# Row loads of late full tiles, and the zeros behind the expert lists: other waits, another order

## The chip, the core and the metric

The kernel runs on one core of a Trainium2 chip. The metric is the device time of one execution in microseconds (us). TensorE is called PE here, VectorE DVE, ScalarE ACT, GpSimd POOL and SyncE SP, as the profile calls them. SP computes nothing in this kernel: its instruction queue issues most of the loads. POOL's queue issues the indirect (scattering) transfers.

## The reference, cut to what matters

One layer: a graph attention step over 4096 tokens of width 256 with a dense 4096 x 4096 adjacency, and then a mixture of 8 experts of which each token uses 2.

```
x = x + gat(layernorm(x), adj, ...)                     # 4 heads of 64, softmax over masked rows
xf = layernorm(x)
top_w, top_i = top_k(xf @ Wg + bg, 2);  top_w = softmax(top_w)
w_dense = sum(one_hot(top_i, 8) * top_w)
for e in range(8):
    h = gelu(xf @ W1[e] + b1[e])                        # 256 -> 1024
    out = out + w_dense[:, e] * (h @ W2[e] + b2[e])     # 1024 -> 256
x = x + out
```

The kernel does not multiply every token by every expert. It sorts tokens into one list for each expert and computes only those rows.

## The kernel before, in words

**Two stages.** The first stage is the attention. It goes over the tokens in four groups of 1024 rows (R). When a group's attention is summed, its rows are finished (residual, layer norm, gate), and each row is written twice, once into the list of each of its two experts. The lists lie in one DRAM tensor, `lists`, with a fixed stretch for each expert; a row is 256 values and four numbers (two weights, the token, the first expert). These writes are indirect DMAs from POOL at L1364, eight for a block of 512 tokens. The rows of the last group are not finished in the first stage: their two blocks (`last_block`) are interleaved, piece by piece, with the first expert tiles of the second stage, by `between`.

**Tiles of the second stage.** A tile is 256 rows of one expert. There are 27 in the main path, numbered here from 0 in the order of `todo`: 9 "early" tiles (0 to 8), which are full with rows of the first two groups alone; 8 "mid" tiles (9 to 16), full with rows of the first three groups alone; 8 "final" tiles (17 to 24), one for each expert, with up to 512 rows; and 2 more. Which expert and which place in its list a tile has is computed on the chip (`plan_early`, `plan_mid`, `plan_rest`), so SP loads a register from a table (L540) before it issues a load.

**One tile.** `fetch` issues three loads on SP: the second bias (L1767, 128 KB), the first weights w1 (L579 or `load_first`, 1 MB) and the second weights w2 (L1774, 1 MB), each with two buffers. `turn` transposes the rows (PE L586) and prepares indices and shares (DVE L1799 to L1816). `up` multiplies with w1 into 8 groups (PE L1848) and applies gelu (ACT L1852). `down` multiplies with w2 (PE L1882), scales (DVE L1895) and adds two blocks of 128 rows to the output by an indirect DMA on POOL (L1907).

**Row loads.** `load_full(k)` loads the 260 KB of rows of tile k on SP (L548, tile name `early`), into one of ROOM = 10 buffers. Tile 0 has its own buffer. Loads 1 to 10 are issued ahead of the loop over tiles. In the loop, iteration i of 2 or more issues the next: load 11 in iteration 2, up to load 16 in iteration 7. A row load waits by hand for every list write that is in `listed` when it is written down, and the framework also makes it wait for every earlier write to the `lists` tensor that was not declared independent.

**Zeros.** The final tiles read past the end of their lists, so zeros are written behind each list. `plan_rest`, reached in iteration 4 when the second last block is listed, writes all eight (POOL L497 to L502, 520 KB each) one after the other.

**Order.** [...] SP's queue holds, for each iteration, the loads of the tile ahead and one late row load, so a row load that waits holds up the weights behind it.

Of the kernel before, what the change touches and what calls it, by code (L numbers as in the profile page):

```python
# [29 lines left out]
CH = P  # L30
TT = 2 * CH
WT = 4 * CH
FINAL = (16, 15, 15, 15, 13, 13, 12, 9)
LIST = 36 * CH
# [10 lines left out]
def gat_then_moe(  # L45
# [19 lines left out]
    nc = tc.nc  # L65
    N, D = x.shape
    H, _, K = W.shape
    E, _, F = W1.shape
# [5 lines left out]
    HB = 2  # L74
# [4 lines left out]
    EARLY, BOTH = (-(-(2 * (N - k * R) - E * (TT - 1)) // TT) for k in (2, 1))  # L79
# [3 lines left out]
    ROOM = 10  # L83
# [5 lines left out]
    TB = B // P  # L89
# [17 lines left out]
    lists = nc.dram_tensor("lists", [E * LIST, RW], F32, kind="Internal").ap()  # L107
# [18 lines left out]
    token = numbers("token", [P, NT], [[P, NT]], step=1)  # L126
# [92 lines left out]
    def forward(apart, stack):  # L219
# [123 lines left out]
        early, mid, rest, final, over = tables("e", EARLY), {}, {}, {}, {}  # L343
# [95 lines left out]
        def plan_rest():  # L439

            plans[0] = kept
            rest.update(tables("r", LATE))
            n = moe_tile("nr", [P, E])
            nc.vector.tensor_tensor(n, filled, starts, OP.subtract)
            left = moe_tile("left", [P, E])
            nc.vector.scalar_tensor_tensor(
                left, used, -float(TT), n, op0=OP.mult, op1=OP.add
            )

            tiles = whole("r", left, TT - 0.5)  # L450
            nc.vector.tensor_scalar(tiles, tiles, -1.0, 0.0, op0=OP.add, op1=OP.max)
            plan(rest, LATE, n, tiles, used)
            nc.vector.tensor_tensor(used, used, tiles, OP.add)
            plan_final(n)
            counts = moe_tile("counts", [P, E + 3])
            above = counts[:, 3:]
            for i in range(E):
                nc.vector.tensor_scalar(
                    above[:, i : i + 1], final["rows"][:, i : i + 1], FINAL[i] * Q + 0.5, None,
                    op0=OP.is_gt,  # L460
                )
            nc.vector.tensor_copy(counts[:, 0:1], rest["upto"][:, E - 1 :])
            nc.vector.tensor_copy(counts[:, 2:3], strayed)
            more = moe_tile("more", [P, 2])
            nc.vector.tensor_scalar(more[:, 0:1], counts[:, 0:1], SURE + 0.5, None, op0=OP.is_gt)
            nc.vector.tensor_reduce(more[:, 1:2], counts[:, 2:], AX.X, OP.max)
            nc.vector.tensor_reduce(counts[:, 1:2], more, AX.X, OP.max)
            nc.vector.tensor_copy(count, counts)


            for t, name, chunks in (rest, "r", 2), (final, "f", 4):
                width = t["own"].shape[1]
                spare = moe_tile(f"spare{name}", [CH, width, chunks])
                nc.vector.tensor_copy(spare, inside[:, 0:1].unsqueeze(2).to_broadcast(spare.shape))
                theirs = moe_tile(f"theirs{name}", [CH, width])
                nc.vector.tensor_tensor(
                    t["past"], t["own"], others.unsqueeze(1).to_broadcast([CH, width, E]), OP.mult
                )
                nc.vector.tensor_reduce(theirs, t["past"], AX.X, OP.add)
                nc.vector.tensor_scalar(theirs, theirs, inside[:, 0:1], None, op0=OP.subtract)  # L480
                new = moe_tile(f"new{name}", [CH, width])
                nc.vector.tensor_scalar(new, t["place"], 0.0, None, op0=OP.is_equal)
                nc.vector.scalar_tensor_tensor(
                    new, t["expert"], float(E), new, op0=OP.is_lt, op1=OP.mult
                )
                nc.vector.tensor_tensor(theirs, theirs, new, OP.mult)
                nc.vector.tensor_tensor(
                    spare[:, :, :2], spare[:, :, :2],
                    theirs.unsqueeze(2).to_broadcast([CH, width, 2]), OP.add,
                )  # L490
                t["spare"] = spare
            zeros = moe_tile("zeros", [CH, WT // CH * RW])
            nc.gpsimd.memset(zeros, 0.0)
            ends = moe_tile("ends", [1, E], I32)
            nc.vector.tensor_copy(ends, filled[0:1, :])
            for e in range(E):
                end = nc.values_load(  # L497
                    ends[0:1, e : e + 1], engines=[mybir.EngineType.Pool],
                    min_val=e * LIST, max_val=e * LIST + N,
                    skip_runtime_bounds_check_because="a list holds each token at most once",  # L500
                )
                nc.gpsimd.dma_start(  # L502
                    lists[bass.ds(end, WT), :].rearrange("(p c) d -> p (c d)", p=CH), zeros
                )

        listed = []

        def after(ins, other, reason):
            tc.add_manual_dep(
                ins, other.name,  # L510
                mybir.DependencyInfo(mybir.DependencyClass.Sync, mybir.DependencyReason.DATA),
                reason=reason,
            )
# [28 lines left out]
                min_val=0, max_val=top, skip_runtime_bounds_check_because=why,  # L542
            )

        def load_rows_of(t, i, xr):
            rows = TT
            first = entry(t, 1, i, E * LIST - WT)
            ins = nc.sync.dma_start(  # L548
                xr, lists[bass.ds(first, rows), :].rearrange("(c p) d -> p c d", p=CH)
            ).ins  # L550
            for i in listed:
                after(ins, i, "rows of the tile")

        def rows_of_job(t, i):
            return FINAL[i] * Q if t is final else TT
# [38 lines left out]
        with ExitStack() as layer:  # L594
# [109 lines left out]
            sums = gat.tile([P, DC, NB], F32)  # L704
# [865 lines left out]
            def fresh():  # L1570

                last[0] = None
                listed.clear()

            def load_mask(a, j):
# [12 lines left out]
            if not apart:  # L1588

                with tc.tile_pool(name="gen", bufs=2) as work:  # L1590
# [12 lines left out]
                    for b in range(NB):  # L1603
                        mine = range(b * B, (b + 1) * B)
                        rows, top = er0[:, 0], er0[:, 1]
                        load_rows(er0[:, :1], b, 1, nc.scalar)
                        nc.vector.memset(top, -BIG)
                        for j in range(NT):
                            if j % 2 == 0:
                                at = load_adj(work, mine, j, 2, 2)  # L1610
# [15 lines left out]
                        for j in range(NT):  # L1626
                            if j % 2 == 0:
                                at = load_adj(work, mine, j, 2, 2)
# [115 lines left out]
        full_rows = [xr0]  # L1744
# [116 lines left out]
        def down(job, hT):  # L1861
# [26 lines left out]
            def give(k, size, po):  # L1888

                if job["last"]:  # L1890
                    o = kept.tile([CH, D], F32, name=f"o_last{k}")
                    last_sums.append(o)
                else:
                    o = work.tile([CH, D], F32, tag="o", name="o", bufs=2 * LAG - 3 if apart else 2)
                given_out.append(nc.vector.scalar_tensor_tensor(  # L1895
                    o[:size], po[:size], share[:size, k : k + 1], b2s[k][:size],
                    op0=OP.mult, op1=OP.add,
                ).ins)
                add = partial(
                    nc.gpsimd.indirect_dma_start, job["into"],  # L1900
                    bass.IndirectOffsetOnAxis(ap=ids[:size, k : k + 1], axis=0), o[:size], None,
                    compute_op=OP.add,
                )
                if job["last"]:
                    held_back.append(add)
                else:
                    add()  # L1907

            full, some = divmod(job["rows"], CH)
            split = some in (Q, 2 * Q)  # L1910
# [39 lines left out]
        def between(n):  # L1950
            if n == 0:
                begun.append(turn_sums(ud))
            for half in range(HB):
                if n == 2 * half:
                    begun.append(last_block(
                        b0 + half, u[:, half], begun[0][:, :, :, half], given[half],
                        xe[:, ts(half, TB)],
                    ))
                if n >= 2 * half and ordered[0]:
                    if next(begun[1 + half], "end") == "end" and half == HB - 1:  # L1960
                        ordered[0] = False
                        plan_rest()
# [8 lines left out]

        def load_full(i):
            xr = work.tile([CH, 2, RW], F32, tag="early", name="early", bufs=ROOM)
            load_rows_of(*((early, i) if i < EARLY else (mid, i - EARLY)), xr)
            full_rows.append(xr)

        for i in range(1, ROOM + 1):
# [7 lines left out]
        for i in range(len(todo)):  # L1985
            if i + 1 == len(jobs) and i + 1 < len(todo):
                jobs.append(fetch(*todo[i + 1]))
            nxt = jobs[i + 1] if i + 1 < len(todo) else None
            if i >= 2 and len(full_rows) < BOTH:
                load_full(len(full_rows))  # L1990
            hT = up(job, xT)
            between(2 * i)
            if nxt:
                xT = turn(nxt)
            giving = down(job, hT)
            next(giving)
            if nxt:
                next(giving, None)
            between(2 * i + 1)
            job = nxt  # L2000

        def held(k, top):
# [82 lines left out]
```

## Time and profile before

| | us |
|---|---|
| three runs | 1273.26, 1274.16, 1278.91 |
| median | 1274.16 |
| the profiled execution | 1281.52 |
| its span, first to last instruction | 1279.9 |
| attention stage, in the span | 0 to about 782 |
| expert tiles, in the span | about 782 to 1276 |

PE is busy for 97% of the span, DVE for 66%, ACT for 35% and POOL for 18%. The DMA engines moved 190.22 MB at a mean of 149 GB/s. In the profile a number such as L548 is a line of the kernel; "SPq" and "POOLq" are the instruction queues of SP and POOL, in which waits and issues of DMAs are recorded.

### The profile page before, as it was taken

To read this page: it belongs to the slowest core of one execution; us is meant where nothing else is said; L and a number is where in the kernel's file an instruction comes from. 1 tells how busy PE (TensorE), PEld (TensorE's weight loads), DVE (VectorE), ACT (ScalarE), POOL (GpSimd) and SP (SyncE) were. 2 spreads that over 40 slices of the span, in tenths; PEclk is the share of its full clock that TensorE was granted. 3 is DMA by queue.
4 is the path that set the end of the run, shared out by engine and by line. 5 is a ranking of instruction groups with operands and counts; after the bars stand their busy time and mean duration, and the time that the engine had idled before them with its cause. 6 is when DMAs were issued, how large, how long until landed. Compare 5 with 4: busy or idle time off the path is not lost.

```text
span 1279.9 us, 22496 instructions
## 1 busy us (share of the span) xinstructions
PE 1247.8 (97%) x8916; PEld 654.9 (51%) x8916; DVE 842.5 (66%) x1566; ACT 451.4 (35%) x929; POOL 235.0 (18%) x217
## 2 busy tenths in 40 slices
PE   8999999999999999999999999999699999999997
PEld 5444444332233322322334326887588886667676
DVE  7998887979999899999999985924011121111120
ACT  4332322165431465322644313432133332222322
POOL 4000000001004210016010051244222221222222
PEclk9999999999999999999999999999799999999999
DMA  6334433536434647335564325857866685555662
GB/s 211 116 116 153 128 100 105 193 83 174 151 105 121 209 106 210 109 97 175 134 195 125 118 72 184 255 161 236 252 177 164 192 211 130 105 113 126 139 148 46
DMA packets 131603, 190.22 MB, mean 149 GB/s; under 512 B 45560, under 2 KB 101744, under 8 KB 131104
## 3 DMA queue, kind: packets, MB, share of 16 engines
q1 hardware_dynamic: 109456, 145.39, 37.7%
q0 software_dynamic: 20544, 36.74, 13.0%
q10 hardware_dynamic: 1488, 6.55, 1.4%
q8 instruction: 72, 1.18, 0.4%
q14 instruction: 43, 0.35, 0.1%
HBM read 155.77 MB, written 29.74 MB: 145 GB/s over the span
## 4 chain that ended last, share of the span: by engine, by line
PE 90%; DVE 4%; issue 2%; DMA 2%; ACT 1%; POOL 1%; POOLq 1%; SPq 0%; DVEq 0%; ACTq 0%
PE acc L1177 33%; PE po L1882 17%; PE den L1186 16%; PE ph L1848 16%; PE pr L1032 2%; DVE w L1667 2%; PE ph L1080 2%; POOL lists L1364 1%; DMA w<-in_L_ffn_W 1%; PE pt L586 0%; PE ptx L1232 0%; DMA early<-lists 0%; PE acc L873 0%; DMA lists<-zeros 0%; PE pt L759 0%
## 5 line engine op out<-in xcount | busy, mean ns | idle before, releaser
L1177 PE MATMUL acc<-w,ha 128*32 128x512 f32 x4096 | 671.7, 593 | 2.5 <-issue 1.2
L1667 DVE SCALAR_TENSOR_TENSOR w<-er,eb,am 128x1024 f32<-128x1024 f32 x496 | 606.0, 1277 | 36.7 <-PE den L1186 30.3
L1186 PE MATMUL den<-w,unit 128*2 128x512 f32 x2048 | 467.4, 592 | 0.4 <-issue 0.3
L1177 PEld LDWEIGHTS acc<-w,ha 128*32 128x32 f32 x4096 | 186.4, 110 | 293.9 <-issue 254.5
L1584 ACT ACTIVATE am<-adj 128x1024 bf16<-128x1024 int32 x124 | 130.6, 1054 | 347.2 <-DVE w L1667 212.6
L1848 PE MATMUL ph<-xT,w 128*128 128x256 f32 (+5 forms) x864 | 232.7, 426 | 16.0 <-DMA w<-in_L_ffn_W 14.7
L1882 PE MATMUL po<-w,hT 128*128 128x256 f32 (+1 forms) x1040 | 229.7, 379 | 0.0
L1852 ACT ACTIVATE hT<-ph,bias 128x256 f32<-128x256 f32 (+5 forms) x216 | 111.1, 517 | 302.5 <-PE ph L1848 190.4
L1882 PEld LDWEIGHTS po<-w,hT 128*128 128x128 f32 (+1 forms) x1040 | 194.9, 189 | 30.7 <-issue 3.4
L1848 PEld LDWEIGHTS ph<-xT,w 128*128 128x128 f32 x864 | 164.3, 191 | 77.5 <-issue 40.0
L1895 DVE SCALAR_TENSOR_TENSOR o<-po,share,b2s 128x256 f32<-128x256 f32 (+2 forms) x66 | 31.8, 483 | 220.8 <-PE po L1882 185.3
L1186 PEld LDWEIGHTS den<-w,unit 128*2 128x2 f32 x2048 | 94.5, 85 | 148.3 <-issue 139.8
L1907 POOL DMA_INDIRECT out<-o,ids x66 | 101.9, 1543 | 339.5 <-DVE o L1895 137.5
L1364 POOL DMA_INDIRECT lists<-xe,at x64 | 83.6, 1306 | 265.5 <-issue 183.3
L590 DVE COPY xT<-pt 128x256 f32<-128x256 f32 x12 | 5.1, 424 | 56.0 <-PE pt L586 56.0
L1832 DVE STREAM_TRANSPOSE xT<-xr 128x960 f32<-128x960 f32 (+5 forms) x10 | 10.0, 1005 | 32.1 <-PE ph L1848 31.2
L1032 PE MATMUL pr<-wr,xT 128*128 128x256 f32 x128 | 30.4, 381 | 0.2 <-ACT er L1126 0.2
L1870 ACT ACTIVATE b2s<-b2b,share 128x256 f32<-128x256 f32 x68 | 30.2, 502 | 0.0
L1420 POOL DMA_DIRECT2D xf<-in_x x6 | 8.1, 1347 | 107.0 <-ACT xf L1419 107.0
L1100 POOL DMA_DIRECT2D residual<-rb x6 | 4.7, 784 | 121.2 <-DVE rb L1047 121.2
L1032 PEld LDWEIGHTS pr<-wr,xT 128*128 128x128 f32 x128 | 24.1, 190 | 5.4 <-issue 0.9
L1080 PE MATMUL ph<-wall,xT 128*128 128x264 f32 x96 | 24.6, 399 | 0.0
(391 smaller groups left out, 654.0 us busy)
## 6 DMA issues: line engine op xcount, KB each, us to landing
adj<-in_adj SPq DMA_DIRECT2D x126, 512.0 KB
w<-in_L_ffn_W SPq DMA_DIRECT2D x54, 1024.0 KB
er<-parts ACTq DMA_DIRECT2D x3, 2048.0 KB
early<-lists SPq DMA_DIRECT2D x16, 260.0 KB
lists<-zeros POOLq DMA_DIRECT2D x8, 520.0 KB
residual<-rb POOLq DMA_DIRECT2D x8, 512.0 KB
rb<-residual SPq DMA_DIRECT2D x8, 512.0 KB
out<-y POOLq DMA_DIRECT2D x8, 512.0 KB
```

Source lines behind the costliest of these rows:

```text
L1032: order_of(nc.tensor.matmul(pr[:, k, :], turned[b][:, c, ts(t0 + k, P)], wr[:, c, :], start=(c == 0), stop=(c == DC - 1),))
L1080: order_of(nc.tensor.matmul(phs[t - t0], xT[:, c, ts(t, P)], wall[:, c, :], start=(c == 0), stop=(c == DC - 1),))
L1177: queue(nc.tensor.matmul(acc[half][h // 2][here : here + Q, :], ha[:, j, h * K + g * Q : h * K + (g + 1) * Q], w[half][h], start=(j == 0), ...
L1186: queue(nc.tensor.matmul(den[here : here + HB, :], unit[:, j, h, 1 - half : 1 - half + HB], w[half][h], start=(j == 0 and half == 0), stop ...
L1364: ins = nc.gpsimd.indirect_dma_start(lists, bass.IndirectOffsetOnAxis(ap=at[:, k, t : t + 1], axis=0), xe[:, t, :], None,).ins
L1584: nc.scalar.activation(am, at, AF.Relu, scale=2.0)
L1667: marks["w"] = nc.vector.scalar_tensor_tensor(wh[:, these], er[:, these, h], eb[:, j, h : h + 1], mask[:, these], op0=OP.max, op1=OP.min,).ins
L1848: order_of(nc.tensor.matmul(ph, job["w1"][:, c, ts(f, P)], xT[:, c, :], start=(c == 0), stop=(c == DC - 1),))
L1852: job["gelu"] = nc.scalar.activation(hT[:, f, :], ph, AF.Gelu, bias=job["bias"][:, f : f + 1]).ins
L1882: order_of(nc.tensor.matmul(po[:size], hT[:, f, k * CH : k * CH + size], w2[:, f, :], start=(f == 0), stop=(f == FC - 1),))
L1895: given_out.append(nc.vector.scalar_tensor_tensor(o[:size], po[:size], share[:size, k : k + 1], b2s[k][:size], op0=OP.mult, op1=OP.add,).ins)
L1907: add()
```

## The change

Three edits go together.

1. A row load above number 10 is "late". It waits for `earlier`, the list writes of the third group alone, and is declared independent of the list writes of the last group and of the zeros.
2. The late loads start one iteration sooner: load 11 is issued in iteration 1, load 16 in iteration 6.
3. `plan_rest` no longer writes the zeros itself. It leaves eight pieces of work in `tails`; the loop takes one at the end of each iteration, so in iterations 4 to 11. Each is put on POOL behind the last output sum issued so far.

```
@@ plan_rest
-            for e in range(E):
-                end = nc.values_load(
...
-                nc.gpsimd.dma_start(
-                    lists[bass.ds(end, WT), :].rearrange("(p c) d -> p (c d)", p=CH), zeros
-                )
+            tails.extend(partial(tail_cleared, ends, zeros, e) for e in range(E))
+        tails = []
+        def tail_cleared(ends, zeros, e):
+            end = nc.values_load(
...
+            clearing.append(nc.gpsimd.dma_start(
+                lists[bass.ds(end, WT), :].rearrange("(p c) d -> p (c d)", p=CH), zeros
+            ).ins)
+            tc.add_manual_dep(
+                clearing[-1], added[-1].name,
...
+                reason="one list for each tile, behind its sums",
+            )
+        clearing, added = [], []
-        listed = []
+        listed, earlier = [], []
@@ load_rows_of
-        def load_rows_of(t, i, xr):
+        def load_rows_of(t, i, xr, late=False):
...
-            for i in listed:
-                after(ins, i, "rows of the tile")
+            if late:
+                for i in earlier:
+                    after(ins, i, "rows of the tile")
+                for i in listed + clearing:
+                    tc.declare_no_dep(ins, i.name, reason="rows behind those of the tile")
+            else:
+                for i in listed:
+                    after(ins, i, "rows of the tile")
@@ fresh
                 last[0] = None
+                earlier.extend(listed[-2 * HB * TB :])
                 listed.clear()
@@ give
-                    add()
+                    added.append(add().ins)
@@ load_full
-            load_rows_of(*((early, i) if i < EARLY else (mid, i - EARLY)), xr)
+            load_rows_of(*((early, i) if i < EARLY else (mid, i - EARLY)), xr, i > ROOM)
@@ the loop over tiles
-            if i >= 2 and len(full_rows) < BOTH:
+            if i and len(full_rows) < BOTH:
                 load_full(len(full_rows))
...
             between(2 * i + 1)
+            if tails:
+                tails.pop(0)()
             job = nxt
```

More of the change, by code (lines that the diff above doesn't have):

```diff
@@ L495, in plan_rest @@
             nc.vector.tensor_copy(ends, filled[0:1, :])
-            for e in range(E):
-                end = nc.values_load(
-                    ends[0:1, e : e + 1], engines=[mybir.EngineType.Pool],
-                    min_val=e * LIST, max_val=e * LIST + N,
-                    skip_runtime_bounds_check_because="a list holds each token at most once",
-                )
-                nc.gpsimd.dma_start(
-                    lists[bass.ds(end, WT), :].rearrange("(p c) d -> p (c d)", p=CH), zeros
-                )
-        listed = []
+            tails.extend(partial(tail_cleared, ends, zeros, e) for e in range(E))
+        tails = []
+        def tail_cleared(ends, zeros, e):
+            end = nc.values_load(
+                ends[0:1, e : e + 1], engines=[mybir.EngineType.Pool],
+                min_val=e * LIST, max_val=e * LIST + N,
+                skip_runtime_bounds_check_because="a list holds each token at most once",
+            )
[4 more added lines that the diff above has]
+                clearing[-1], added[-1].name,
+                mybir.DependencyInfo(mybir.DependencyClass.NoSync, mybir.DependencyReason.DATA),
+                reason="one list for each tile, behind its sums",
+            )
+        clearing, added = [], []
+        listed, earlier = [], []
         def after(ins, other, reason):
```

## The prediction

> **What bounds the kernel now.** I read the page first: which engine is full, and where it is not.
>
> ```profile
> PE 1247.8 (97%) x8916; PEld 654.9 (51%) x8916; DVE 842.5 (66%) x1566; ACT 451.4 (35%) x929; POOL 235.0 (18%) x217
> PE   8999999999999999999999999999699999999997
> PEclk9999999999999999999999999999799999999999
> ...
> L1848 PE MATMUL ph<-xT,w 128*128 128x256 f32 (+5 forms) x864 | 232.7, 426 | 16.0 <-DMA w<-in_L_ffn_W 14.7
> ```
>
> PE is full in every slice of 32 us except the one from 896 us on, where its granted clock falls too. The group of the first expert product (L1848) names one wait of 14.7 us, for weights. Restricted to 908 us and later, PE's waits hold this one entry and no other, so everything after it moves with it. Next I followed the chain that ended last through that hole.
>
> ```profile
> 893.87 5.45 DMA lists<-zeros
> 899.69 0.38 SPq L548
> 900.12 0.27 SPq L540
> 900.64 0.35 SPq L1767
> 901.03 0.27 SPq L540
> 901.55 6.94 DMA w<-in_L_ffn_W
> 908.53 8.83 PE ph L1848 x32
> 917.36 6.91 PE po L1882 x32
> ```
>
> Read upwards: PE starts tile 7 at 908.53 when its w1 lands; SP issued that load at 901.55, behind the tile's bias (L1767), behind a row load (L548) issued at 899.69, which waited for the last zeros to land. SP's own waits give its length:
>
> ```profile
> SPq L548 <- DMA lists<-zeros: 32.8, 1, 32.8
> SPq L548 <- DMA lists<-xe,at: 6.4, 1, 6.4
> ```
>
> These are loads 14 and 13. From SP's timeline (L548 issued at 815.87, 831.71, 862.92, 899.69, 903.11, 908.26) loads 11 and 12 did not wait for list writes; load 13 waited for the first last block's writes, load 14 for the zeros. Nothing on POOL makes PE late by itself: the zeros are a false neighbour of the weights in SP's queue.
>
> Last, stretches of about a tile, with PE, PEld, DVE, ACT and POOL busy, then the clock:
>
> ```profile
> 893.00:909.00 16.00, 1.31 (x8) 1.05 (x7) 1.48 (x8) 0.37 (x1) 3.72 (x3) 0.66 0.76 236
> 909.00:924.00 15.00, 15.00 (x64) 12.92 (x64) 0.48 (x1) 4.84 (x11) 3.10 (x2) 0.90 0.93 303
> 938.00:953.00 15.00, 15.00 (x73) 13.22 (x72) 2.50 (x10) 4.85 (x11) 4.40 (x3) 1.00 0.72 173
> ```
>
> The hole costs twice: no work in it, and a clock of 0.90 in the next stretch (tile 7's 32 matmuls take 8.83 us, those of later tiles 6.91).
>
> [...] the trace has 8.83 - 6.91 = 1.92, which I use.
>
> **The change, part by part.**
>
> *Late loads lose their waits.* In the compiled program's list of waits, loads 11 to 16 now wait only for their buffer (a DVE instruction) and for an earlier DMA of SP. What then issues tile 7's w1? The bias in front of it needs the buffer of tile 5's bias, free when ACT has scaled it twice (L1870, 870.07 + 0.92 = 870.99). From the bias's issue to w1's is 0.9 us in this trace (900.64 to 901.55), so w1 goes at about 872.0 and, with 6.94 us, lands at about 879. PE needs it when the product before ends, 893.02 (the six transposes until 893.84 are work that has to be done in either kernel). So 14 us of cover. w2 of tile 7 waits for tile 5's second product (876.6), is due at about 900.5 and has 17 us to spare. Saved: idle 893.84 to 908.53 = 14.69 us, and the slow restart, 1.92. Sum 16.61.
>
> *What is late next?* Nothing that this trace shows: load 14 goes at about 848 (after tile 5's w2 at 847.08), load 15 at about 863 (after tile 6's w2) and load 16 at about 877.5 (after tile 7's w2); the rows whose buffers they take (tiles 4, 5 and 6) are read by DVE L1816 by 832, 849 and 865.5, and they belong to tiles that start 100 us or more later.
>
> *Loads one iteration sooner.* Six loads, the same number. Load 11 moves ahead of tile 3's loads on SP: one register load and one issue, about 0.9 us, in the stretch at 805, and 260 KB more in front of w1 of tile 3 (issued 808.17, due at 831.09): hidden. Loads 12 to 16 each take the place in SP's queue that the load before them had, and take the buffer of the tile transposed one iteration earlier, where it was two: load 12 (about 815.9) needs tile 2's rows read, which DVE L1816 ends at 803.94, so 12 us to spare; load 13 (about 831.2) needs tile 3's, read at 821.94, 9 us. If DVE were over 9 us late, SP would stand, and behind it tile 5's bias (held anyway until 841.20) and w1. Cost: nothing.
>
> *Zeros one a tile.* The same eight register loads, eight issues and 4.16 MB. On POOL the eight took 885.01 to 894.40, 1.17 us each; two output sums a tile take 2 x 1.85 with the gap. That is 4.9 us of a tile of 14.25, and the sums' buffers (9) cover more than four tiles. Without that cover it would be 8 x 1.17 = 9.4 us. The first clear still waits 2.4 us for list writes. The second and third gain a wait, for loads 15 and 16, which are to have landed by about 868 and 882, ahead of these clears (about 892 and 901). Behind a waiting clear on POOL stand the next tile's sums, and DVE waits for those only nine sums later. On the DMA engines a clear is 520 KB, 1.3 us at 400 GB/s (the rate in the burst of zeros), beside a w1 with 14 us of cover. Cost: nothing.
>
> *Final tiles.* Their first load (L562) now waits for the eighth clear. It stands behind tile 11's sums: 983.40 before, so 966.8 after; issued by 969.6, landed by 975.0 with the 5.45 us of before. SP reaches L562 at 1024.78 - 16.61 = 1008.2. Cover 33 us.
>
> *Not counted.* In tile 6's first product ACT's gelus come 1.45 us apart instead of 0.86 (from 879.80 on), and the product takes 9.25 us instead of 6.99. The trace shows no cause. Before, this was hidden, since the hole ended when w1 came; after, it may stay (value 0, which I take) or be gone (2.3 us more saved). If such a stretch came anew elsewhere it would cost as much: 0 to 2.3 both ways.
>
> Against the profiled execution: 1281.52 - 16.61 = 1264.9, span 1263.3. The median is 7.36 us below that execution. I take the hole as equal in the timed runs, so 1274.16 - 16.61 = **1257.6**.
>
> **Rivals.** *The hole is smaller without the profiler.* The profiled execution is 7.36 us longer than the median, and nothing says where. For: POOL issues many small transfers just here. Against: the hole's end is a chain of landings on DMA, and the 782 us of attention leave more room for 7 us. If all of it lay in the hole, the gain would be 9.25: 1264.9.
>
> *The wait moves.* Another load on SP or a clear on POOL holds PE. For: SP and POOL stay in order, and each late load has one tile less of room. Against: the covers of 14 and 17 us for tile 7's weights and of 9 us for load 13. With half the hole left, 8.3 us gained: 1265.9.
>
> *Slower: the final tiles wait for the last clear.* Place: SP at L562 of tile 17. If each clear holds POOL's queue behind the sums, the eighth lands late, and from 33 us late on SP stands; PE follows after at most another 27 us (L562 at 1024.78, PE at 1051.89). To lose 6.4 us net it must eat 16.61 as well: some 83 us late in the far case, 56 in the near one, 7 to 10 us a clear against 1.17 measured. Time then 1280.6 or more. For: one in-order queue with everything in it. Against: POOL idles most of every tile.
>
> *The change does nothing*: a wait that the framework adds by itself would remain. The compiled waits speak against it: 1274.
>
> **How the numbers follow.** A difference of 0.5% (6.4 us) is about what a measurement of this kernel can tell from none. Chances: the full hole (gain 14 to 19.5 us) 0.80; more than that 0.04; a smaller hole or a moved wait with 6.4 to 14 us gained 0.09; within 0.5% 0.04; slower 0.03. Faster is 0.80 + 0.04 + 0.09 = 0.93. The likeliest case alone, with 2.3 us up and down and 1 to 2 us for the medians, gives 1254 to 1261. The range goes on to 1252.5 for more gain and 1265 for half of the smaller-hole cases.
>
> **What would show it.** Right: PE's slices all at 9 until the end; no PE wait for w above 1 us after 782; no SP wait at the row load for zeros or list writes; w1 of tile 7 issued near 872, its matmuls 6.9 us; eight L507 issues about 14 us apart from 885 to 970; span near 1263. Wrong: a PE hole elsewhere after 800, a wait on SP at L580 (the final tiles' load, L562 before) with PE idle behind it, or POOL's sums with DVE waiting for them.

## The result, and the profile after

| | before | after | ratio after/before, 95% interval |
|---|---|---|---|
| first comparison: median us (runs) | 1275.20 (6) | 1263.03 (6) | 0.9898 [0.9868, 0.9929] |
| repeated later | 1282.33 (19) | 1265.55 (6) | 0.9876 [0.9857, 0.9895] |
| repeated once more | 1282.29 (29) | 1265.70 (4) | 0.9875 [0.9847, 0.9904] |
| repeated on another chip | 1274.42 (11) | 1259.60 (6) | 0.9886 [0.9865, 0.9907] |
| the profiled execution (span) | 1281.52 (1279.9) | 1259.90 (1258.2) | |

The change is faster by 12.2 us in the first comparison (9.1 to 16.8 by its interval), and by 14.8 to 16.8 in the repeats. The sum of the prediction was 16.6, and its forecast for the median 1257.6. In the two profiled executions the difference is 21.6.

The page of the changed kernel, first the busy times of the engines, then the two rows of 40 slices, then the group of the first expert product:

```profile
PE 1243.7 (99%) x8916; PEld 650.9 (52%) x8916; DVE 842.8 (67%) x1566; ACT 451.6 (36%) x929; POOL 240.2 (19%) x217
...
PE   9999999999999999999999999999999999999997
...
PEclk9999999999999999999999999999999999999999
...
L1867 PE MATMUL ph<-xT,w 128*128 128x256 f32 (+5 forms) x864 | 229.9, 423 | 0.2 <-ACT hT L1871 0.2
```

The slice at 896 us that held a 6 is a 9 and its clock is full. The product that stood 16.0 us before its matmuls stands 0.2 us, for gelu and no longer for weights. The longest and the last of PE's waits from 782 us on (us in total, times, longest; the three between them are of 0.5, 0.5 and 0.3 us):

```profile
PE pt L604 <- ACT xT L1253: 0.6, 2, 0.3
...
PE ph L1867 <- ACT hT L1871: 0.2, 1, 0.2
```

No entry is for weights, and nothing took the hole's place. How that came about is in SP's timeline (start, length, instruction):

```profile
861.20 0.38 SPq L560 DMA_DIRECT2D early<-lists  x1
868.05 0.34 SPq L1786 DMA_DIRECT2D b2b<-in_L_ffn_b  x1
868.95 0.37 SPq L597 DMA_DIRECT2D w<-in_L_ffn_W  x1
873.83 0.37 SPq L1793 DMA_DIRECT2D w<-in_L_ffn_W  x1
874.95 0.30 SPq L560 DMA_DIRECT2D early<-lists  x1
1003.27 0.37 SPq L580 DMA_DIRECT2D known<-lists  x1
```

Loads 15 and 16 (L560) go at 861.20 and 874.95, each in its turn, and the weights of tile 7 at 868.95 and 873.83. SP waits for zeros nowhere. PE's timeline shows no gap at tile 7 (the second product of tile 6, then the first of tile 7):

```profile
880.98 7.07 PE L1901 MATMUL po<-w,hT 128*128 128x256 f32 x32
887.88 7.07 PE L1867 MATMUL ph<-xT,w 128*128 128x256 f32 x32
```

And the first two of the stretches that the prediction showed, now full at a clock of 1.00 (length, then PE, PEld, DVE, ACT, POOL busy with their counts, clock, DMA share, GB/s):

```profile
893.00:909.00 16.00, 16.00 (x78) 14.06 (x77) 2.15 (x9) 5.79 (x13) 4.99 (x4) 1.00 0.85 254
909.00:924.00 15.00, 15.00 (x75) 13.23 (x74) 2.21 (x10) 5.35 (x13) 4.63 (x5) 1.00 0.90 228
```

**Where 21.7 us of span went.** The expert tiles, from tile 0's first product (781.67 before, 778.56 after) to the end of the span, take 498.2 us before and 479.6 after, so 18.6 less. The attention ends 3.1 us sooner. These 3.1 have nothing to do with the change: in two later profiles of the changed kernel the first product starts at 783.51 and 783.25, later than before. Of the 18.6, 14.69 are the hole and 1.76 its slow restart (tile 7's first product is 8.83 long in PE's timeline before and 7.07 after), and 2.17 are a slow stretch in tile 6 that the prediction had left out at value 0: from the start of its first product to the start of its second is 9.52 us before (876.59 to 886.11) and 7.35 after.

### The profile page after: what moved, and what is told of

It is laid out like the page before. It is cut to its first block, busy times and chain, and to the rows that moved or that the text cites. A ratio compares the mean times of both kernels' runs of the same rounds, so it can differ in the third digit from the quotient of the medians.

```text
span 1258.2 us, 22490 instructions
## 1 busy us (share of the span) xinstructions
PE 1243.7 (99%) x8916; PEld 650.9 (52%) x8916; DVE 842.8 (67%) x1566; ACT 451.6 (36%) x929; POOL 240.2 (19%) x217
## 4 chain that ended last, share of the span: by engine, by line
PE 94%; DVE 3%; issue 1%; DMA 1%; ACT 1%; POOLq 0%; SPq 0%; DVEq 0%; ACTq 0%
PE acc L1195 33%; PE po L1901 18%; PE ph L1867 17%; PE den L1204 17%; PE pr L1050 2%; DVE w L1686 2%; PE ph L1098 2%; PE pt L604 1%; PE ptx L1250 0%; DMA early<-lists 0%; PE acc L891 0%; PE pt L777 0%; PE ptr L1488 0%; PE po L1940 0%; PE pl L1261 0%
## 5 line engine op out<-in xcount | busy, mean ns | idle before, releaser
L1867 PE MATMUL ph<-xT,w 128*128 128x256 f32 (+5 forms) x864 | 229.9, 423 | 0.2 <-ACT hT L1871 0.2
L1382 POOL DMA_INDIRECT lists<-xe,at x64 | 88.1, 1377 | 267.3 <-issue 184.3
```

The source lines that it names most:

```text
L1382: ins = nc.gpsimd.indirect_dma_start(lists, bass.IndirectOffsetOnAxis(ap=at[:, k, t : t + 1], axis=0), xe[:, t, :], None,).ins
L1867: order_of(nc.tensor.matmul(ph, job["w1"][:, c, ts(f, P)], xT[:, c, :], start=(c == 0), stop=(c == DC - 1),))
```

## The experiments

The theory: the one row load that waits at SP for the last zeros, with tile 7's weights behind it, is the whole of the gain. The rivals: a part comes from spreading the zeros, or from issuing loads sooner; or the change has an effect at some other place. Runs compared in one paragraph share a chip, unless the text says otherwise.

**The changed kernel again, and each edit alone.** The first four runs take the changed kernel once more and its three edits one at a time. The changed kernel again (its profile is in the table of stages below):

> The changed kernel once more, beside the kernel before. Theory (the hole is 16.6 us with or without the profiler, and the shortfall of the first measurement is spread between executions): 14 to 18.5 us below the kernel before, profile without a PE wait for weights. Rival (the hole is smaller when no profile is taken, or PE without a pause gets a lower clock): 10 to 13 us below, with a granted clock of 0.996 or less in the longer runs where the kernel before has more.

Measured: 1265.55 against 1282.33, ratio 0.9876 [0.9857, 0.9895], 16.8 us gained. The rival's lower clock does not show: the six runs of the changed kernel here have a mean granted clock of 0.995 to 0.999, the 19 of the kernel before 0.989 to 0.995, and in the first comparison the changed kernel has 0.996 to 0.999.

Only the waits are removed. The zeros stay in one burst in `plan_rest` (here `tail_cleared` without its order behind the sums, called eight times in a row), and the loads keep their iterations:

```diff
             for e in range(E):
...
+                tail_cleared(ends, zeros, e)
...
+            if late:
+                for i in earlier:
+                    after(ins, i, "rows of the tile")
+                for i in listed + clearing:
+                    tc.declare_no_dep(ins, i.name, reason="rows behind those of the tile")
...
-            load_rows_of(*((early, i) if i < EARLY else (mid, i - EARLY)), xr)
+            load_rows_of(*((early, i) if i < EARLY else (mid, i - EARLY)), xr, i > ROOM)
```

> The kernel before with only the waits of late loads taken away; zeros in one burst as before, loads not started sooner. Theory (the wait on SP is the whole cause): the same time as the changed kernel, within 2 us, no PE wait for weights. Rival (spreading the zeros is needed too, since the burst of 4.16 MB slows the weights behind it): a PE wait of 3 us or more between 890 and 915 us, and 5 to 12 us more than the changed kernel.

Measured: 1264.82, ratio 0.9876 [0.9853, 0.9899], against 0.9876 for the whole change. SP's timeline, then POOL's with the first and the last of the eight zeros:

```profile
871.74 0.35 SPq L1782 DMA_DIRECT2D b2b<-in_L_ffn_b  x1
872.66 0.37 SPq L593 DMA_DIRECT2D w<-in_L_ffn_W  x1
```

```profile
889.66 0.58 POOL L508 DMA_DIRECT2D lists<-zeros  x1 [4.56 <-DMA lists<-xe,at]
...
897.34 0.53 POOL L508 DMA_DIRECT2D lists<-zeros  x1 [0.74 <-issue]
```

The burst of zeros is still there and POOL still waits 4.56 us before it, while PE's product of tile 7 begins at 892.61, in the middle of the burst, on weights that were issued at 872.66. So the waits alone are the cause, within the 3 us either way that the interval leaves, and a burst of 4.16 MB beside the tiles costs PE nothing that shows (tile 7's product is 7.07 us long). Tile 8's w1, issued at 889.49 into the burst, was there when its product was due at 906.87; how far zeros and weights slow each other where they overlap, no run here measures. On POOL the burst does hold what stands behind it: tile 6's first sum, whose values DVE has ready at 889.90, goes at 898.26, behind the eighth write.

Only the zeros are spread, one for each tile. Late loads still wait for every list write and every zero written down ahead of them:

```diff
-            for e in range(E):
...
+            tails.extend(partial(tail_cleared, ends, zeros, e) for e in range(E))
...
+            if tails:
+                tails.pop(0)()
```

> The kernel before with only the zeros written one list for each tile; late loads still wait, loads not started sooner. Theory: load 14 waits for the first list's zeros alone, SP goes on near 890 us instead of 899.7, the weights of tile 7 land near 899, and a PE hole of 5 to 7 us with a slow restart remains: 7 to 11 us below the kernel before. Rival (the burst is the cause, not the wait): the full gain, 14 us or more. Second rival (the waits return one by one for each later list): no gain, several PE holes.

Measured: 1273.91, ratio 0.9929 [0.9904, 0.9954], 8.4 us gained. The chain of work that ended last (start, length, what) is the old one with a shorter first link:

```profile
885.96 4.02 DMA lists<-zeros
...
890.31 0.38 SPq L560
...
892.16 6.64 DMA w<-in_L_ffn_W
...
898.93 9.77 PE ph L1867 x32
```

Load 14 waits for one write of zeros where it had waited for eight. SP is released some 9 us sooner than in the kernel before (890.31 for 899.69), and PE starts 8.6 us after it, as it did before (8.8). PE's hole is 7.64 us, a little over the 5 to 7 expected. The second rival, that waits return for the later lists, is true of SP and not of PE:

```profile
SPq L560 <- DMA lists<-zeros: 22.6, 3, 9.6
```

SP waits three times, and PE stands only behind one of the three. What this edit gains is gained through the same wait.

Only the start of the loads is moved:

```diff
-            if i >= 2 and len(full_rows) < BOTH:
+            if i and len(full_rows) < BOTH:
```

> The kernel before with only the late loads started one iteration sooner. Theory: load 15 stands where load 14 stood in SP's queue and waits for the zeros just as long; the hole stays within 1 us, the time within 2 us of the kernel before. Rival (one load fewer behind the zeros is enough): 5 us or more below.

Measured: 1281.38, ratio 0.9992 [0.9982, 1.0002]. SP's longest wait and PE's:

```profile
SPq L548 <- DMA lists<-zeros: 32.5, 1, 32.5
```

```profile
PE ph L1848 <- DMA w<-in_L_ffn_W: 15.7, 1, 15.7
```

Load 14 goes one iteration sooner, but load 15 then stands where 14 stood, and the wait is whole. By itself this edit does nothing.

**The slower rival, brought about.** If the zeros come late enough, the first load of the final tiles (L580) must hold SP. They are put off by four tiles:

```diff
-            if tails:
+            if tails and i >= 8:
                 tails.pop(0)()
```

> The changed kernel with its eight zero writes taken from iteration 8 on instead of iteration 4, so about 57 us later, the last one in iteration 15. Theory (the final tiles' first load waits for the last zeros, and PE stands when it comes later than the cover): the last zeros land near 1039 us in the profile against SP's arrival near 1003, SP waits about 36 us there, tile 17's w1 lands some 11 us less than that late, a PE hole of 20 to 28 us with a slow restart, 22 to 30 us slower than the changed kernel. Rival (the cover is larger or the wait is not there): within 2 us of the changed kernel.

Measured: 1275.41 (1273.16 to 1285.79), ratio to the kernel before 0.9958 [0.9933, 0.9984]. Against the changed kernel beside it (1265.70) it loses 9.7 us. The mechanism is there, in SP's waits and in PE's timeline of tile 17; the last fence is PE's timeline of the changed kernel at the same product:

```profile
SPq L580 <- DMA lists<-zeros: 20.2, 1, 20.2
```

```profile
1052.36 16.84 PE L1867 MATMUL ph<-xT,w 128*128 128x512 f32 x32 [6.90 <-DMA w<-in_L_ffn_W]
```

```profile
1035.33 13.90 PE L1867 MATMUL ph<-xT,w 128*128 128x512 f32 x32
```

6.90 of hole and 16.84 - 13.90 = 2.94 of slow restart make 9.8. The loss expected, 22 to 30, was missed. It supposed the eighth write four tiles (57 us) later than in the changed kernel. There, the write runs behind a backlog: it went at 976.98, 17.83 us after tile 12's first product began (959.15), since POOL's sums ran about a tile late after the list writes. Put off, it went at 1034.51, only 3.0 us after tile 16's (1031.49), because by then the backlog was gone: some 42 us later in place of 57. In this profile it was gone early, after tiles 5 and 6, in which PE stood (tile 6's first sum goes at 900.78, while its second product runs). In two profiles of the changed kernel tile 15's second sum still comes 9.6 and 12.2 us behind the start of tile 16 (1025.77 for 1016.16, 1033.72 for 1021.51), where it comes 2.0 behind here (1033.52). So a part of the missing 15 us may belong to this execution.

The profiled execution, 1285.79, is 10 us above the median of its kernel; tiles 5 to 7 run some 12 us late in it, long before any zeros, with 7.3 us of PE's waits on gelu. One more of its seven runs is as long (1284.34). That part stays open. The hole is the one loss that the placing of the zeros explains, and it is as large as the medians' difference; the shorter runs have no profile to show that theirs is the same.

> The changed kernel a third time, to see whether 12.2 us (first measurement) or 16.8 us (second) is the rule. Theory (16.6 us of the sum, and up to 2.3 more for tile 6's stretch that the hole had hidden): 14 to 19 us below the kernel before. Rival (a smaller hole in the timed runs): 10 to 13 us.

This is the changed kernel beside it; its ratio is in the first table.

**Why two comparisons gave 16.7 us and one 12.2.** The repeats above were taken on a chip where the kernel before needs 1282.3, and the first comparison found 1275.2. So the kernel before was profiled again, there and elsewhere.

> The kernel before against itself. A ratio of 1.000 within 0.002, and a profile with the same hole: 14 to 17 us of PE wait for weights and a product of 8.5 to 9.8 us behind it. If the hole differs by more than 3 us between executions, the first measurement's shortfall can come from there.

Measured: 1282.61 against 1282.29 for the same kernel, ratio 1.0004 [0.9994, 1.0013]. The hole is 15.3 us and the product behind it 9.60 long, as expected. On another chip, the changed kernel and then, on a third, the kernel before in two executions:

> The changed kernel a fourth time; another chip where there is one. Theory: 14 to 19 us below the kernel before, as in the second and third measurement. Rival: 10 to 13 us as in the first, if that difference belongs to the chip rather than to chance in few runs.

Measured: 1259.60 against 1274.42, 14.8 us.

> The kernel before, one look, for the hole in another execution. Theory: hole and slow product behind it together 16 to 19 us in every execution, whatever the attention stage took. If an execution without the pause at the end of attention (DVE idle for 5 to 7 us before its last two products, near 765 us) has a hole of 12 to 15 us, the smaller gains of the first and fourth measurement come from there.

> The same once more: hole and slow product together 16 to 19 us (theory) or, in an execution without the pause at the end of attention, 12 to 15 us.

Measured: 1271.26 and 1274.91, single executions, beside 1273.48 for a third one. PE's wait at tile 7 in the run of before repeated on the first chip, and in these two:

```profile
PE ph L1848 <- DMA w<-in_L_ffn_W: 15.3, 1, 15.3
```

```profile
PE ph L1848 <- DMA w<-in_L_ffn_W: 10.0, 1, 10.0
```

```profile
PE ph L1848 <- DMA w<-in_L_ffn_W: 11.0, 1, 11.0
```

The hole itself is smaller in these executions: with the slow restart 11.8 and 12.7 us, so the 16 to 19 us of the theory do not hold in every execution; the other reading, 12 to 15, was met at its low end. They differ from the others in one more thing, at the end of the attention. DVE's timeline at its last pairs of attention products, for the kernel before as recorded with the prediction, for the kernel before on the third chip, and for the changed kernel (in brackets the idle time ahead, and what ended it):

```profile
770.57 2.48 DVE L1667 SCALAR_TENSOR_TENSOR w<-er,eb,am 128x1024 f32<-128x1024 f32 x2 [6.46 <-remote]
```

```profile
763.94 2.48 DVE L1667 SCALAR_TENSOR_TENSOR w<-er,eb,am 128x1024 f32<-128x1024 f32 x2 [0.27 <-PE den L1186]
```

```profile
765.91 2.48 DVE L1686 SCALAR_TENSOR_TENSOR w<-er,eb,am 128x1024 f32<-128x1024 f32 x2 [0.27 <-PE den L1204]
```

In the first, DVE stands for 6.5 us ahead of the same pair, and PE does less: from 765 to 772 us it has 25 matmuls there and 68 in the second. This pause of DVE of 5.0 to 7.2 us is in all seven profiles from the first chip of the repeats, of either kernel and of the variants, and in the recorded profile of before; it is in neither of the last two profiles of before, nor in the changed kernel's first profile, nor in its profile from the other chip. So it belongs to the execution or the chip and not to the change. The recorded profile of before had it, while the runs of before timed with it (1273 to 1279) are as short as those without. That is the likely home of the 7.36 us between that profile and the median; the unprofiled runs have no trace to show it.

**All stages on one table.** The stage of tiles (tile 0's first product to the end of the span), what PE loses in it at tile 7 (the restart is the length of the product behind the hole in PE's timeline, over the 7.07 of a smooth one), and the slow gelu stretches of tiles 5 and 6 (time from the start of the first product to that of the second, over the 7.43 us of a smooth tile 5 or the 7.35 of a smooth tile 6); the last column was taken before rounding:

| profile | pause | stage, us | hole | slow restart | tiles 5, 6 | stage less these |
|---|---|---|---|---|---|---|
| before, recorded | yes | 498.2 | 14.7 | 1.8 | 2.2 | 479.6 |
| before, repeated | yes | 497.7 | 15.3 | 2.5 | 0 | 479.8 |
| start alone | yes | 497.4 | 15.7 | 2.1 | 0 | 479.6 |
| before, third chip | no | 493.0 | 10.0 | 1.8 | 1.1 | 480.1 |
| before, third chip | no | 496.4 | 11.0 | 1.7 | 3.0 | 480.7 |
| zeros alone | yes | 490.1 | 7.6 | 2.7 | 0 | 479.8 |
| waits alone | yes | 480.6 | 0 | 0 | 1.0 | 479.6 |
| changed, first profile | no | 479.6 | 0 | 0 | 0 | 479.6 |
| changed, repeated | yes | 479.6 | 0 | 0 | 0 | 479.6 |
| changed, repeated | yes | 480.4 | 0 | 0 | 0.8 | 479.5 |
| changed, another chip | no | 480.4 | 0 | 0 | 0 | 480.4 |

The last column is the same to 1.1 us in eleven profiles of five kernels, and what is left lies in tile 0: from the start of its first product to that of the second it takes 10.4 to 10.9 us in the three profiles above 480, and 9.8 to 10.1 in the others. So the hole, its restart and the slow stretches are all there is: nothing else in the tiles moved. The stage of the changed kernel is 17 to 19 us shorter than before's where before paused, and 13 to 17 where it did not. The comparisons gained 12.2 to 16.8.

**Why the hole differs.** The hole lies between two moments, the one when PE is due and the one when the weights land. PE is due at tile 7 some 112 us after tile 0's start (112.2 in the recorded profile; 121.68 - 10.04 = 111.6 in the first one on the third chip, which is compared here). The weights come when the zeros let SP go, and that was 117.6 us after tile 0 in the recorded profile and 113.7 on the third chip; w1 then landed in 6.94 and 5.80 us. 3.9 + 1.1 sooner, less the 0.5 by which PE too was due sooner, is the difference of the holes, 14.7 - 10.0, to 0.2 us. SP's wait for zeros is shorter too, 27.6 us on the third chip for 32.8. The 3.9 can be seen on POOL. Two sums stand ahead of the last block's list writes; here are both, in the recorded profile of before and then on the third chip:

```profile
863.32 1.60 POOL L1907 DMA_INDIRECT out<-o,ids  x1 [2.22 <-DVE o L1895]
870.72 1.58 POOL L1907 DMA_INDIRECT out<-o,ids  x1 [5.80 <-DVE pastf L396]
```

```profile
856.96 1.60 POOL L1907 DMA_INDIRECT out<-o,ids  x1 [0.31 <-issue]
861.64 1.58 POOL L1907 DMA_INDIRECT out<-o,ids  x1 [3.08 <-DVE share L1813]
```

Counted from tile 0's start, the first sum goes 1.3 us sooner in the second profile and the second sum 4.0. The second sum follows the first by 7.4 us in one and 4.7 in the other. The profile names a DVE instruction that has nothing to do with sums; a sum waits for the one before to land (of the sums' waits in the kernel before, 21 with 96.9 us together are put to `out<-o,ids`), and in the long case tile 6's two weight loads, issued at 864.75 and 865.40, are under way at the same time. That they slow it is argued from the order of issue; no run took the loads away. All twelve profiles fit it: the sums are 7.4 to 9.2 us apart in the nine where a weight load was issued between 3.0 us before the first sum and 1.5 after it, and 4.6 to 4.7 in the three where none was. The other profile from the third chip adds a second reason. Its hole of 11.0 is smaller because the zeros let SP go sooner, 116.0 us after tile 0's start for 117.6, and about as much because PE came 1.9 later to it, behind a longer tile 0 and longer slow stretches in tiles 5 and 6. What such a stretch takes off the hole is no gain of the change.

## Why the prediction was right, and which term was off

**The removed wait: right.** Tile 7's w1 was forecast at 872.0 with tile 0 at 781.67. It went at 868.95 with tile 0 at 778.56, which is 872.06 on the same scale. PE never waited for it. w2 was due to be issued at 876.6 and went at 873.83 + 3.11 = 876.94. That the removed waits carry the whole gain is shown by the run with only them: the same ratio as the whole change, 0.9876, each with an interval of 2 to 3 us either way.

**The slow restart: right in kind, with a slip in the reading.** The term was 8.83 - 6.91 = 1.92. But 8.83 is the length of a product and 6.91 the distance from one product to the next; a smooth product is 7.07 long in PE's timeline, so the recorded restart is 1.76. The runs gave 1.7 to 2.9, for holes of 6.9 to 15.7 us, with no proportion to the hole (2.9 and 2.7 behind the shortest two, 1.8 behind the recorded 14.7).

**The edits costed at nothing: right.** Loads one iteration sooner, alone: 1.0 us less (2.3 less to 0.3 more by the interval). Zeros one a tile: the whole change and the waits alone have the same ratio. But the zeros came later than forecast. The second and third writes went at 896.16 and 909.36, which is 899.3 and 912.5 on the scale of before, where about 892 and 901 were written, and the last at 976.98, which is 980.1 on that scale, 10.5 us later than the 969.6 of the sum:

```profile
896.16 1.17 POOL L507 DMA_DIRECT2D lists<-zeros  x1
...
909.36 0.59 POOL L507 DMA_DIRECT2D lists<-zeros  x1
...
976.98 1.17 POOL L507 DMA_DIRECT2D lists<-zeros  x1
```

The step had set the clear behind tile 11's sums at the times of before less the hole; POOL's sums lag by most of a tile behind the list writes, a backlog that the hole had given POOL time to work off. The lag was covered: PE's group of the first product waited 0.2 us in all, and no wait of DVE from 782 us on is for a sum.

**The final tiles' cover: right in kind, 11 us too large.** With 4.3 us for issue and landing (the delay measured in the run with late zeros, 1034.51 to 1038.79), the last zeros land at about 981.3, and SP reaches L580 at 1003.27: 22 us of cover, where 33 stood. The run with late zeros gives the second half of the margin: SP stood 20.2 us and PE only 6.9, so 13.3 us more lie between SP and PE, where the prediction had at most 27. The slower rival begins about 35 us later than the changed kernel puts the last zeros.

**The stretch of tile 6: the value 0 was wrong for the recorded execution, the bound right.** It was put at 0 to 2.3 us. It is 2.2 in the recorded profile and gone in the changed kernel's first one, yet it is absent from two profiles that still have the waits (before repeated, start alone), and 1.0 and 0.8 us of it are in two with the waits gone. It comes and goes by execution; no run showed its cause. So of the 18.6 us 16.4 were the change's, and the rest came with the two executions.

**The term that was off: the size of the hole.** The prediction says "I take the hole as equal in the timed runs". 14.69 was the hole of one execution, the paused one, which was 7.36 us above the median. In the two profiles of before without the pause it was 10.0 and 11.0; with the restart that is 11.8 and 12.7 in place of 16.6. The first rival had the direction right, that the hole could be smaller in the timed runs, and a gain of 9.25 was its far end; its ground, the profiler, is not supported, since profiles of before on the third chip have the small hole too. The argument against it was the step that failed: that the hole ends with "a chain of landings on DMA" was taken to make it steady. The end of that chain is just what varied, by 3.9 us at the zeros and 1.1 at w1. That pause and long hole go together rests on five profiles of before and its one-edit variant, three with and two without, and the two without are also the only ones from their chip; why is open.

**Whether this is why the first comparison gained only 12.2 is not shown.** With a gain of 12 to 13 the forecast would have been about 1262, near the measured 1263.03. But the timed runs have no trace, and three things speak for caution. The interval of the first comparison, 9.1 to 16.8, still takes in the 16.6. On the chip where before is as short as there (1274.42), the gain was 14.8. And the six runs of the changed kernel in the first comparison fall into two groups, 1258.3 to 1261.6 and 1264.4 to 1266.6: the first is as long as its runs on that other chip (1258.6 to 1263.0), the second about as long as those on the chip where every profile has the pause (1264.8 to 1269.3). If three of the six runs had the pause, that alone would take some 3 us off the gain (a median of 1263.03 for the 1259.9 in the middle of the first group).

So the number was met in part by luck. 1263.03 lies outside the 1254 to 1261 that the likeliest case alone was given, and a gain of 12.2 belongs by its size to the case "a smaller hole or a moved wait", which had a chance of 0.09. The three repeats, with 14.8 to 16.8, belong to the full hole, which had 0.80.

The wait did not move, and the framework left no wait of its own: both rivals fall with PE's list of waits above.

## What to carry to other kernels

A load that waits holds what stands behind it in its queue (here 32.8 us, with tile 7's weights behind), so the cost of a false dependence is found by asking what stands behind it and when that was due; and if one removed wait explains the gain, run it alone, since edits that seem to belong to it may bring nothing. A hole that begins where the engine is due and ends where a load lands has no fixed size (10.0 to 15.3 us in four profiles of one kernel): before its length goes into a sum against a median, look whether the profiled execution is one of the long ones, and take the length from several profiles if it is. Subtract like from like: a length from a length, a distance between starts from another. When work is put off on a queue, count from the queue's own backlog and not from the stage that it is named after.

## What the runs showed of the hardware that was not expected

- The same kernel took 1282.3 us on one chip (29 runs) and 1274.4 on another (11 runs). The changed kernel took 1265.6 and 1259.6. The pause at the end of the attention was in every profile of the first chip. In it DVE stands for 5.0 to 7.2 us, and the profile names no cause that explains it ("remote" in six profiles, a transposition on PE in two); POOL writes lists at that time in paused and in unpaused profiles, so that alone is not the cause, and none was found.
- A write of 520 KB of zeros on POOL, beside full tiles, released a waiting load 4.3 us after its issue; eight of them in one burst left PE's product at its smooth 7.07 us.
- The restart behind a hole cost 1.7 to 2.9 us in seven holes of 6.9 to 15.7 us, and not more behind the longer ones.
